# Two f32 stages of a perceiver layer in three passes of split operands, on one Trainium2 core

## The chip, the cores and the metric

The kernel runs on one core of one Trainium2 chip. The metric is the device time of one execution in microseconds; three executions of the kernel before gave 2127.59, 2129.59 and 2129.66 us, so the median is 2129.59.

## What is computed

A perceiver layer: 128 rows of 512 attend to 12544 context rows with 16 heads of 128, then pass a linear attention with a decay per head, then a feed-forward of ternary weights. Each of the three is added to its own input.

```python
def xattn(xn, ctx, Wq, Wk, Wv, Wo):            # H = 16, HD = 128
    q = (xn @ Wq).reshape(b, sq, H, HD) * (1.0 / np.sqrt(HD))
    k = (ctx @ Wk).reshape(b, skv, H, HD)
    v = (ctx @ Wv).reshape(b, skv, H, HD)
    attn = softmax(einsum('bqhd,bkhd->bhqk', q, k))
    return einsum('bhqk,bkhd->bqhd', attn, v).reshape(b, sq, H * HD) @ Wo

def attn(xn, log_decay, Wq, Wk, Wv, Wo, Wg1, Wg2, norm_w):   # 16 heads of 32
    q, k, v = silu(xn @ Wq), silu(xn @ Wk), silu(xn @ Wv)
    o = lightning_attn(q, k, v, log_decay)     # one chunk of 128: (q k^T * D) v
    o = o * sigmoid((xn @ Wg1) @ Wg2)
    return (rms_normed_by_head(o) * norm_w) @ Wo

x = x + xattn(layernorm(x), ctx_2048, ...)
x = x + attn(layernorm(x), ...)
x = x + ffn(layernorm(x), ...)                 # act_quant, ternary w1 and w2
```

## The kernel before

The cross attention is done without ever forming k and v. Wk is multiplied into q first, so that the scores come from the context itself (first loop, line 190), and Wv is applied last, to the weighted sums of the context (`uT`). Both loops hold their f32 operands as two parts: a high part rounded to fp32r by a copy on ScalarE, and a low part, which is the difference, by a subtraction on VectorE. A product is then three fp32r matmuls, low by high, high by low and high by high, added up in PSUM.

The first loop writes the scores to DRAM (`sc_d`), in two halves `f` of the heads. The second loop (the `for k` loop around line 700) takes 2 x 98 = 196 steps. Step k works on one half of a block of 256 context rows: TensorE runs `weigh` for step k (24 matmuls of 512 columns, line 469), while ScalarE and VectorE prepare steps k+1 to k+3: `high_part` and `low_part` (lines 523 and 528), `cut_hi` and `cut_lo` for the context (505, 511), `soften` (517, 518) and the running sum `total` (536). Three buffers for `ph` and `pl` let the preparation run ahead by up to two steps. `load_scores(k + 5)` and `load_ctx(k + 4)` are issued on SyncE's queue.

Work that belongs to no step is put into the loop by `at(k, job)`. The ternary weights of the feed-forward are made there (`stage`, `magnitude`, `quantize`), in four tiles `kq1_0` to `kq1_3` that stay in SBUF until the feed-forward. The weights Wv and Wo of the cross attention are loaded in four groups each, into the rooms `kq1_4` to `kq1_6` in turn, or into score buffers (pool `io`).

After the loop the order of each engine is fixed by hand: `seq` keeps the instructions that it marks in the program's order on their engine. `values(g)` (line 742) multiplies a group of four heads with Wv, in f32, and scales it by the inverse sums into `cT` (line 752). `outs(g)` (line 763) multiplies it with Wo, in f32, 256 columns at a time, onto `po`. The order on TensorE is values 0 and 1, outs 0, values 2, outs 1, values 3, outs 2, outs 3. Beside it VectorE takes the reciprocals of the sums of the second half (line 774), and ScalarE makes the decay matrix (line 799) from `df`, which GpSimd's iota starts (line 793). Then x1 = po + x0 (line 832), its layer norm, its transposition, the three projections of the linear attention in f32 (q and k with the weights stationary, so that they come out transposed, line 853; v at 876), the gate (870, 879), the scores by head (890), the identity matmul that puts x1 under the last sum (897), the weighted values `po2` (906), the gated norm, Wo (932, 935) and the feed-forward. `keep_warm(n)` puts n matmuls of zeros on TensorE where it would stand idle.

Of the kernel before, what the change touches and what calls it, by code (L numbers as in the profile page):

```python
# [8 lines left out]
F32 = mybir.dt.float32  # L9
F32R = mybir.dt.float32r  # L10
BF16 = mybir.dt.bfloat16
# [5 lines left out]
P = 128  # L17
# [16 lines left out]
def tile_perceiver_layer(  # L34
# [546 lines left out]
    w1q = [kq1p.tile([P, 2, FF], BF16, name=f"kq1_{n}") for n in range(2)]  # L581
    w2q = [kq1p.tile([P, 8, D], BF16, name=f"kq1_{n + 2}") for n in range(2)]
    parts = const.tile([P, 2, 8], F32, name="parts")
    staged = {}
# [44 lines left out]

    def score_tile(shape):  # L630

        return iop.tile(shape, F32, tag="io", name="wt")

    def by_cols(w, g, room=weight_tile):

        t = room([P, NC, 512])
        nc.sync.dma_start(out=t, in_=w[:, g * 512 : (g + 1) * 512].rearrange("(c p) e -> p c e", p=P))
        return t

    def by_rows(w, g, room=weight_tile):  # L640

        t = room([P, 4, D])
        nc.sync.dma_start(out=t, in_=w[g * 512 : (g + 1) * 512, :].rearrange("(h p) d -> p h d", p=P))
        return t

    wv, wo = {}, {}
    jobs = {}

    def at(k, job, *args):
        jobs.setdefault(k, []).append((job, args))  # L650
# [18 lines left out]
    for q in range(8):  # L669
        at(2 * NP + 10 + 3 * q, lambda q: seq(nc.vector.reciprocal(rl[0][:, q * P : (q + 1) * P], rl[0][:, q * P : (q + 1) * P])), q)  # L670
    at(2 * NP + 40, lambda: wv.update({0: by_cols(x_wv, 0)}))
    at(2 * NP + 44, lambda: wv.update({1: by_cols(x_wv, 1)}))
    at(2 * NP + 48, lambda: wo.update({0: by_rows(x_wo, 0)}))
    at(4 * NP - 4, lambda: wv.update({2: by_cols(x_wv, 2, score_tile)}))
    at(4 * NP - 3, lambda: wo.update({1: by_rows(x_wo, 1, score_tile)}))

# [59 lines left out]
    def values(g):  # L736
        f, b = g // 2, g % 2
        pc = ps_m.tile([P, G, P], F32, tag="m", name="pc")
        for j in range(G):
            for cc in range(NC):  # L740
                seq(
                    nc.tensor.matmul(  # L742
                        pc[:, j, :],
                        lhsT=wv[g][:, cc, j * HD : (j + 1) * HD],
                        rhs=uT[f][:, cc, b * 512 + j * P : b * 512 + (j + 1) * P],
                        start=(cc == 0),
                        stop=(cc == NC - 1),
                    )
                )
        cTs[g] = work.tile([P, G, P], F32, tag="cT", name="cT", bufs=3)  # L750
        seq(
            nc.vector.tensor_tensor(
                cTs[g].rearrange("p a b -> p (a b)"), pc.rearrange("p a b -> p (a b)"),
                rl[f][:, b * 512 : (b + 1) * 512], ALU.mult,
            )
        )

    def outs(g):
        for half, hs in enumerate(halves):
            for j in range(G):  # L760
                h = g * G + j
                seq(
                    nc.tensor.matmul(  # L763
                        po[half], lhsT=cTs[g][:, j, :], rhs=wo[g][:, j, hs], start=(h == 0), stop=(h == H - 1)
                    )
                )

    ld = small.tile([P, H], F32, tag="ld", name="ld", bufs=1)
    nc.sync.dma_start(out=ld, in_=log_decay.partition_broadcast(P))
    values(0)  # L770
    wv[3] = by_cols(x_wv, 3)
    for q in range(4):
        qs = slice(q * 256, (q + 1) * 256)
        seq(nc.vector.reciprocal(rl[1][:, qs], rl[1][:, qs]))
    values(1)
    wo[2] = by_rows(x_wo, 2)
    outs(0)
    wo[3] = by_rows(x_wo, 3)
    late = [keepp.tile([P, 8, 512], F32, name="uT0")]
    a_w = {"q": by_cols(a_wq, 0, lambda shape: late[0][:, 4:, :])}  # L780
    wg1 = ctp.tile([P, NC, P], F32, tag="hi", name="wg1")
# [8 lines left out]


    di = work.tile([P, P], I32, name="di")
    nc.gpsimd.iota(di, pattern=[[1, P]], base=0, channel_multiplier=-1)
    df = work.tile([P, P], F32, name="df")
    nc.vector.tensor_copy(df, di)
    nc.vector.tensor_scalar_max(df, df, 0.0)
    decay = ctp.tile([P, H, P], F32, tag="raw", name="decay", bufs=1)
    for h in range(H):
        nc.scalar.activation(decay[:, h, :], df, AF.Exp, scale=ld[:, h : h + 1])
    nc.gpsimd.affine_select(  # L800
        out=decay, in_=decay, pattern=[[0, H], [1, P]], compare_op=ALU.is_ge, fill=0.0, base=0, channel_multiplier=-1
    )

    values(2)
    outs(1)
    values(3)
    late.append(keepp.tile([P, 8, 512], F32, name="uT1"))
    a_w["k"] = by_cols(a_wk, 0)
    outs(2)
    a_w["v"] = by_cols(a_wv, 0)  # L810
    outs(3)
    a_w["o"] = by_rows(a_wo, 0)
    rows = {}
# [17 lines left out]
    for half, hs in enumerate(halves):  # L831
        seq(nc.vector.tensor_tensor(x1[:, hs], po[half], x0[:, hs], ALU.add))
        seq(nc.vector.bn_stats(out=st0[:, half, :], in_=x1[:, hs]))
    mv0 = small.tile([P, 2], F32, tag="mv", name="mv0")
    seq(nc.vector.bn_aggr(out=mv0, in_=st0))
# [3 lines left out]
    xa = work.tile([P, D], F32, tag="xa", name="xa")  # L839
    xaT = work.tile([P, NC, P], F32, tag="T", name="xaT", bufs=2)  # L840
    for half, hs in enumerate(halves):
        seq(nc.vector.tensor_scalar(xa[:, hs], x1[:, hs], mv0[:, 0:1], c0, ALU.subtract, ALU.mult))
    for half in range(2):
        transposed(xa, xaT, half)

    def project_T(w):

        pp = ps_m.tile([P, NC, P], F32, tag="m", name="pp")
        for half in range(2):
            for e in range(NC):  # L850
                for cc in (2 * half, 2 * half + 1):
                    seq(
                        nc.tensor.matmul(  # L853
                            pp[:, e, :],
                            lhsT=w[:, cc, e * P : (e + 1) * P],
                            rhs=xaT[:, cc, :],
                            start=(e == 0 and cc == 0),
                            stop=(e == NC - 1 and cc == NC - 1),
                            skip_group_check=True,
                        )  # L860
                    )
        return pp

    qT = late[0][:, 0, :].rearrange("p (e q) -> p e q", e=NC)
    kT = late[1][:, 0, :].rearrange("p (e q) -> p e q", e=NC)
    seq(nc.scalar.activation(qT, project_T(a_w["q"]), AF.Silu))
    seq(nc.scalar.activation(kT, project_T(a_w["k"]), AF.Silu))
    pg = ps_v.tile([P, P], F32, tag="v", name="pg")
    for cc in range(NC):
        seq(nc.tensor.matmul(pg, lhsT=wg1[:, cc, :], rhs=xaT[:, cc, :], start=(cc == 0), stop=(cc == NC - 1)))  # L870
    g1T = work.tile([P, P], F32, tag="g1T", name="g1T")
    seq(nc.vector.tensor_copy(g1T, pg))
    v = late[1][:, 1, :]
    pv = ps_v.tile([P, D], F32, tag="v", name="pv")
    for cc in range(NC):
        seq(nc.tensor.matmul(pv, lhsT=xaT[:, cc, :], rhs=a_w["v"][:, cc, :], start=(cc == 0), stop=(cc == NC - 1)))  # L876
    seq(nc.scalar.activation(v, pv, AF.Silu))
    pgate = ps_v.tile([P, D], F32, tag="v", name="pgate")
    seq(nc.tensor.matmul(pgate, lhsT=g1T, rhs=wg2, start=True, stop=True))
    gate = late[1][:, 2, :]  # L880
    seq(nc.scalar.activation(gate, pgate, AF.Sigmoid))
    seq(nc.scalar.activation(warm, eps_t, AF.Sqrt))


    pscs = [(ps_m, ps_t)[r // 2].tile([P, NC, P], F32, tag="mt"[r // 2], name="psc") for r in range(4)]
    for e in range(NC):
        for r in range(4):
# [6 lines left out]
            )  # L894
    pp = [ps_v.tile([P, 256], F32, tag="v", name="pp") for _ in range(2)]
    for half, hs in enumerate(halves):
        seq(nc.tensor.matmul(pp[half], lhsT=ident, rhs=x1[:, hs], start=True, stop=False))
    po2 = ps_s.tile([P, 512], F32, tag="s", name="po2")
    decayed = decay.rearrange("p (e r) q -> p r e q", r=4)
    for r in range(4):  # L900
        sc = late[1][:, 4 + r, :].rearrange("p (e q) -> p e q", e=NC)
        seq(nc.vector.tensor_tensor(sc, pscs[r], decayed[:, r, :, :], ALU.mult))
        for e in range(NC):

            cs = slice((4 * e + r) * LHD, (4 * e + 4) * LHD)
            seq(nc.tensor.matmul(po2[:, cs], lhsT=sc[:, e, :], rhs=v[:, cs], start=True, stop=True))  # L906
    keep_warm(ps_w, 13)
    og = ctp.tile([P, 2, D], F32, tag="lo", name="og")
# [20 lines left out]
    for i in range(NC):  # L929
        for half, hs in enumerate(halves):  # L930
            if i < 2:
                seq(nc.tensor.matmul(pp[half], lhsT=ogT[:, i, :], rhs=a_w["o"][:, i, hs], start=False, stop=False))  # L932
    for half, hs in enumerate(halves):
        for i in (2, 3):
            seq(nc.tensor.matmul(pp[half], lhsT=ogT[:, i, :], rhs=a_w["o"][:, i, hs], start=False, stop=(i == 3)))
    keep_warm(ps_w, 13)
# [136 lines left out]
    s2, step2 = quant_scales(am5[:, 4:5], others, 1.0)  # L1073
    hq = work.tile([P, FF], BF16, tag="hq", name="hq")
    py = [ps_v.tile([P, 256], F32, tag="v", name="py") for _ in range(2)]
# [94 lines left out]
```

## Time and profile before

| what | us |
|---|---|
| time, median of three | 2129.59 |
| the profiled execution, its time | 2127.83 |
| its span in the profile | 2126.1 |
| TensorE busy | 2112.7 |
| VectorE busy | 1646.7 |
| ScalarE busy | 754.2 |
| first matmul of `values(0)` to the end of `outs(3)` | 2038.96 to 2067.09 |
| first projection matmul to the first of `po2` | 2070.17 to 2085.20 |
| end of the span | 2126.1 |

The page of the profile gives busy time by engine, the span in 40 slices, the costliest groups of instructions (line, engine, operation, tiles, count, busy time, mean of one, idle time before it), and the chain of work that ended last. A matmul's mean is longer than the distance between two of them, since they are pipelined; the distance is read from the chain. An f32 matmul leaves two records, an fp32r one leaves one.

### The profile page before, as it was taken

How to read it: one execution, taken by the hardware profiler on the slowest of the kernel's cores; microseconds unless marked ns; L12 is line 12 of the kernel's file. 1: busy time of each engine (PE TensorE's matmuls, PEld its weight loads, DVE VectorE, ACT ScalarE, POOL GpSimd, SP SyncE). 2: the span in 40 equal slices, each digit the busy share in tenths (PEclk: the TensorE clock that was granted, in tenths of full speed). 3: DMA queues.
4: the chain of work that ended last, by engine and by line, in shares of the span. 5: the costliest groups of instructions: out<-in, count | busy, mean ns of one | idle time of the engine just before them, and what ended most of it. 6: DMA issues, size and time to landing. Idle time of an engine off the chain costs nothing.

```text
span 2126.1 us, 23916 instructions
## 1 busy us (share of the span) xinstructions
PE 2112.7 (99%) x9591; PEld 1745.2 (82%) x9595; DVE 1646.7 (77%) x1827; ACT 754.2 (35%) x846; POOL 25.7 (1%) x15
## 2 busy tenths in 40 slices
PE   8999999999999999999999999999999999999998
PEld 7888888888888888888888888888888888888885
DVE  6877777777777777778897888887788777777745
ACT  6222122211222122214444444444544444444424
POOL 0000000000000000000000000000010000000010
PEclk9999999999999999999999999999999999999999
DMA  5333333333333333336664454553444434444460
GB/s 207 135 140 127 149 141 137 139 129 149 134 144 137 130 149 129 149 151 216 216 238 150 181 179 168 174 202 143 149 149 149 148 142 140 145 142 146 149 230 6
DMA packets 70767, 326.22 MB, mean 153 GB/s; under 512 B 7265, under 2 KB 11617, under 8 KB 45185
## 3 DMA queue, kind: packets, MB, share of 16 engines
q1 hardware_dynamic: 70512, 324.57, 41.4%
q8 instruction: 75, 1.23, 0.2%
q14 instruction: 36, 0.29, 0.1%
q10 hardware_dynamic: 144, 0.13, 0.0%
HBM read 221.65 MB, written 103.02 MB: 153 GB/s over the span
## 4 chain that ended last, share of the span: by engine, by line
PE 98%; DVE 1%; DMA 1%; ACT 0%; SPq 0%; issue 0%; DVEq 0%; ACTq 0%
PE pu L469 50%; PE ps L190 44%; PE pc L742 1%; PE po L763 1%; PE pk L364 1%; DMA kq<-in_x_wq_dram 1%; PE pp L853 0%; PE pq L344 0%; PE po L906 0%; PE pv L876 0%; SPq L300 0%; DVE uT L1057 0%; DVE st L1031 0%; PE pp L932 0%; ACT kq L409 0%
## 5 line engine op out<-in xcount | busy, mean ns | idle before, releaser
L190 PE MATMUL ps<-kq,cth 128*128 128x512 f32 x2744 | 844.5, 389 | 0.0
L469 PE MATMUL pu<-ph,cl 128*128 128x512 f32 x1568 | 610.0, 389 | 0.0
L469 PE MATMUL pu<-pl,ch 128*128 128x512 f32 x1568 | 610.0, 389 | 0.0
L469 PE MATMUL pu<-ph,ch 128*128 128x512 f32 x1568 | 610.0, 389 | 0.0
L190 PEld LDWEIGHTS ps<-kq,cth 128*128 128x128 f32 x2744 | 515.2, 188 | 106.6
L190 PE MATMUL ps<-kq,ctl 128*128 128x512 f32 x1344 | 522.8, 389 | 0.0
L523 ACT CAST ph<-si 128x1024 fp32r<-128x1024 f32 x194 | 203.9, 1051 | 491.9 <-PE pu L469 491.7
L469 PEld LDWEIGHTS pu<-pl,ch 128*128 128x128 f32 x1568 | 294.4, 188 | 61.2
L469 PEld LDWEIGHTS pu<-ph,cl 128*128 128x128 f32 x1568 | 294.4, 188 | 60.9
L469 PEld LDWEIGHTS pu<-ph,ch 128*128 128x128 f32 x1568 | 294.4, 188 | 60.9
L219 DVE TENSOR_TENSOR so<-ps,u 128x512 f32<-128x512 f32 x294 | 202.7, 690 | 134.9 <-PE ps L190 130.5
L190 PEld LDWEIGHTS ps<-kq,ctl 128*128 128x128 f32 x1344 | 252.3, 188 | 52.4
L511 DVE TENSOR_TENSOR cl<-cr,ch 128x1024 fp32r<-128x1024 f32 x98 | 120.2, 1227 | 204.8 <-ACT ch L505 204.8
L254 ACT COPY so<-ps 128x512 f32<-128x512 f32 x98 | 57.6, 588 | 577.6 <-PE ps L190 577.6
L528 DVE TENSOR_TENSOR pl<-si,ph 128x1024 fp32r<-128x1024 f32 x194 | 242.4, 1250 | 1.0 <-ACT ph L523 1.0
L237 DVE TENSOR_TENSOR mx<-mx,so 128x1024 f32<-128x1024 f32 x190 | 232.2, 1222 | 6.7
L517 DVE TENSOR_TENSOR si<-si,mb 128x1024 f32<-128x1024 f32 x194 | 235.7, 1215 | 0.0
L536 DVE TENSOR_TENSOR lsum<-lsum,si 128x1024 f32<-128x1024 f32 x192 | 233.8, 1218 | 0.0
L518 ACT ACTIVATE si<-si 128x1024 f32<-128x1024 f32 x194 | 205.4, 1059 | 60.4 <-DVE si L517 60.4
L505 ACT CAST ch<-cr 128x1024 fp32r<-128x1024 f32 x98 | 102.3, 1044 | 0.0
L176 DVE TENSOR_TENSOR ctl<-ctr,cth 128x1792 fp32r<-128x1792 f32 x47 | 94.9, 2019 | 0.7 <-ACT cth L171 0.7
L171 ACT CAST cth<-ctr 128x1792 fp32r<-128x1792 f32 x48 | 81.7, 1703 | 37.5 <-PE ps L190 35.5
(224 smaller groups left out, 757.8 us busy)
## 6 DMA issues: line engine op xcount, KB each, us to landing
sc<-so SPq DMA_DIRECT2D x98, 1024.0 KB, 3.8
si<-sc SPq DMA_DIRECT2D x97, 1024.0 KB, 5.0
cr<-in_c_dram SPq DMA_DIRECT2D x98, 512.0 KB, 3.5
ctr<-in_cT_dram SPq DMA_DIRECT2D x48, 512.0 KB, 3.5
kq<-in_w1T_dram SPq DMA_DIRECT2D x16, 512.0 KB, 4.3
kq<-in_w2T_dram SPq DMA_DIRECT2D x16, 512.0 KB, 5.0
kq<-in_x_wv_dram SPq DMA_DIRECT2D x3, 1024.0 KB, 5.2
kq<-in_x_wo_dram SPq DMA_DIRECT2D x3, 1024.0 KB, 7.3
```

The costliest lines, as they stand in the source:

```text
L176: return lo, nc.vector.tensor_tensor(lo, raw[:, :7, :, :], hi, ALU.subtract)
L190: nc.tensor.matmul(ps, lhsT=lt[:, a, cc, :], rhs=right(f, b, part)[:, cc, :], start=(first and n == 0), stop=(n == 5), skip_group_check=True,)
L219: place(nc.vector.tensor_tensor(to, t[p], t[q], ALU.add))
L237: place(nc.vector.tensor_tensor(mx[f], mx[f], t["so"][:, j, :], ALU.max))
L469: nc.tensor.matmul(pu[b][cc], lhsT=lt[:, j, cs], rhs=rt[:, bs], start=(first and n == 0), stop=(last and n == 2))
L505: seq(nc.scalar.copy(ctx_hi[f, i], ctx_raw[f, i]))
L511: seq(nc.vector.tensor_tensor(ctx_lo[f, i], ctx_raw[f, i], ctx_hi[f, i], ALU.subtract))
L517: seq(nc.vector.tensor_tensor(exps[k], exps[k], mb[f], ALU.subtract))
L518: seq(nc.scalar.activation(exps[k], exps[k], AF.Exp))
L523: seq(nc.scalar.copy(high[k], exps[k]))
L528: seq(nc.vector.tensor_tensor(low[k], exps[k], high[k], ALU.subtract))
L536: seq(nc.vector.tensor_tensor(lsum[f], lsum[f], exps[k], ALU.add))
```

## The change

Two f32 stages take the form of the loops. `outs` uses the high and the low part of both `cT` and Wo, three fp32r matmuls instead of one f32 matmul. The projections q, k and v use the parts of the transposed x (`xaTh`, `xaTl`) and of their weights, 12 fp32r matmuls of 512 columns each; q and k now come out untransposed, and four transpositions each (`turned`) follow their silu.

The weights are split before they are needed: groups 0 to 2 of Wo inside the second loop (steps 91 to 95, 134 to 138, 142 to 146), group 3 and the three projection weights after it, a quarter (128x512) at a time between the other work of ScalarE and VectorE. The rooms for the parts come from the ternary weights: at step 84 their four tiles are written to DRAM (1 MB each), and they are read back in the stage of the linear attention. The reciprocals of the second half move later, in two pairs; `df` and the decay matrix move earlier; the identity matmul of x1 moves behind `po2`, where seven warm-up matmuls stand instead of 13; `hq` lies in another pool.

```diff
+    ternary_d = [dram.tile([P, 4096], BF16, name=f"ternary{n}") for n in range(4)]
...
+    def ternary(n):
+        return (w1q + w2q)[n].rearrange("p a b -> p (a b)")
+    def put_away(n):
+        nc.sync.dma_start(out=ternary_d[n], in_=ternary(n))
+    def high_quarter(w, hi, lo, q):
+        seq(nc.scalar.copy(hi[q], w[:, q, :]))
+    def low_quarter(w, hi, lo, q):
+        seq(nc.vector.tensor_tensor(lo[q], w[:, q, :], hi[q], ALU.subtract))
+    def quarters(*tiles):
+        return [t[:, q, :] for t in tiles for q in range(4 // len(tiles))]
+    def room(name):
+        return lambda shape, dtype=F32: kq1p.tile(shape, dtype, name=name)
+    def part_in(place):
+        return quarters(place([P, 4, D], F32R))
+    def bring(g, raw_room, hi_room, lo_room):
+        t = by_rows(x_wo, g, raw_room)
+        wo[g] = t, hi_room(), part_in(lo_room)
...
-    at(2 * NP + 40, lambda: wv.update({0: by_cols(x_wv, 0)}))
-    at(2 * NP + 44, lambda: wv.update({1: by_cols(x_wv, 1)}))
-    at(2 * NP + 48, lambda: wo.update({0: by_rows(x_wo, 0)}))
+    for n in range(4):
+        at(84, put_away, n)
+    at(87, lambda: bring(0, room("kq1_4"), lambda: part_in(room("kq1_0")), room("kq1_1")))
+    at(130, lambda: bring(1, room("kq1_5"), lambda: part_in(room("kq1_2")), room("kq1_3")))
+    mx_rooms = lambda: quarters(*[mxp.tile([P, 2, D], F32R, tag=f"mx{n}", name="wh") for n in range(2)])
+    at(137, lambda: bring(2, room("kq1_4"), mx_rooms, room("kq1_6")))
+    for g, k in ((0, 91), (1, 134), (2, 142)):
+        for q in range(4):
+            at(k + q, lambda g, q: high_quarter(*wo[g], q), g, q)
+            at(k + 1 + q, lambda g, q: low_quarter(*wo[g], q), g, q)
+    at(150, lambda: wv.update({0: by_cols(x_wv, 0, room("kq1_5"))}))
+    at(152, lambda: wv.update({1: by_cols(x_wv, 1, room("kq1_4"))}))
     at(4 * NP - 4, lambda: wv.update({2: by_cols(x_wv, 2, score_tile)}))
-    at(4 * NP - 3, lambda: wo.update({1: by_rows(x_wo, 1, score_tile)}))
+    at(4 * NP - 3, lambda: wv.update({3: by_cols(x_wv, 3, score_tile)}))
+    at(4 * NP - 2, lambda: wo.update({3: by_rows(x_wo, 3, lambda shape: ctp.tile(shape, F32, tag="raw", name="w3", bufs=1))}))
...
-        cTs[g] = work.tile([P, G, P], F32, tag="cT", name="cT", bufs=3)
+        cTs[g] = work.tile([P, G, P], F32, tag="cT", name="cT", bufs=1)
...
+    def values_hi(g):
+        hi = work.tile([P, G, P], F32R, tag="Th", name="cTh", bufs=2)
+        seq(nc.scalar.copy(hi, cTs[g]))
+        cTs[g] = hi, cTs[g]
+    def values_lo(g):
+        hi, t = cTs[g]
+        lo = work.tile([P, G, P], F32R, tag="Tl", name="cTl", bufs=2)
+        seq(nc.vector.tensor_tensor(lo, t, hi, ALU.subtract))
+        cTs[g] = hi, lo
     def outs(g):
+        hi, lo = cTs[g]
+        _, whi, wlo = wo[g]
         for half, hs in enumerate(halves):
             for j in range(G):
-                h = g * G + j
-                seq(
-                    nc.tensor.matmul(
-                        po[half], lhsT=cTs[g][:, j, :], rhs=wo[g][:, j, hs], start=(h == 0), stop=(h == H - 1)
+                parts_ = ((lo, whi[j][:, hs]), (hi, wlo[j][:, hs]), (hi, whi[j][:, hs]))
+                for n, (lt, rt) in enumerate(parts_):
+                    seq(
+                        nc.tensor.matmul(
+                            po[half], lhsT=lt[:, j, :], rhs=rt, start=(g == 0 and j == 0 and n == 0),
+                            stop=(g == NG - 1 and j == G - 1 and n == 2),
+                        )
                     )
-                )
...
     ld = small.tile([P, H], F32, tag="ld", name="ld", bufs=1)
     nc.sync.dma_start(out=ld, in_=log_decay.partition_broadcast(P))
-    values(0)
-    wv[3] = by_cols(x_wv, 3)
+    wo[3] = wo[3], part_in(score_tile), None
     for q in range(4):
+        high_quarter(*wo[3], q)
+    di = work.tile([P, P], I32, name="di")
+    nc.gpsimd.iota(di, pattern=[[1, P]], base=0, channel_multiplier=-1)
+    df = work.tile([P, P], F32, name="df")
+    seq(nc.vector.tensor_copy(df, di))
+    seq(nc.vector.tensor_scalar_max(df, df, 0.0))
+    def inverse_sums(q):
         qs = slice(q * 256, (q + 1) * 256)
         seq(nc.vector.reciprocal(rl[1][:, qs], rl[1][:, qs]))
+    values(0)
+    wo[3] = *wo[3][:2], part_in(room("kq1_5"))
+    values_hi(0)
+    low_quarter(*wo[3], 0)
+    values_lo(0)
+    for q in (1, 2):
+        low_quarter(*wo[3], q)
     values(1)
-    wo[2] = by_rows(x_wo, 2)
+    late = [keepp.tile([P, 8, 512], F32, name="uT0")]
+    a_w = {}
+    def split_hi(name, qs=range(4)):
+        for q in qs:
+            high_quarter(*a_w[name], q)
+    def split_lo(name, qs=range(4)):
+        for q in qs:
+            low_quarter(*a_w[name], q)
+    wq_raw = by_cols(a_wq, 0, lambda shape: late[0][:, 4:, :])
+    wk_raw = by_cols(a_wk, 0, room("kq1_4"))
+    low_quarter(*wo[3], 3)
+    values_hi(1)
+    values_lo(1)
+    for h in range(H):
+        seq(nc.scalar.activation(decay[:, h, :], df, AF.Exp, scale=ld[:, h : h + 1]))
...
     outs(0)
-    wo[3] = by_rows(x_wo, 3)
-    late = [keepp.tile([P, 8, 512], F32, name="uT0")]
-    a_w = {"q": by_cols(a_wq, 0, lambda shape: late[0][:, 4:, :])}
+    wv_raw = by_cols(a_wv, 0, room("kq1_0"))
+    a_w["q"] = wq_raw, part_in(room("kq1_1")), None
...
+    inverse_sums(0)
+    inverse_sums(1)
+    split_hi("q")
     values(2)
+    a_w["q"] = *a_w["q"][:2], part_in(score_tile)
+    values_hi(2)
+    values_lo(2)
     outs(1)
+    a_w["k"] = wk_raw, part_in(room("kq1_2")), part_in(room("kq1_3"))
+    inverse_sums(2)
+    inverse_sums(3)
+    split_hi("k")
+    split_lo("q", (0,))
     values(3)
     late.append(keepp.tile([P, 8, 512], F32, name="uT1"))
-    a_w["k"] = by_cols(a_wk, 0)
+    a_w["v"] = wv_raw, part_in(score_tile), None
+    values_hi(3)
+    split_lo("q", (1,))
+    values_lo(3)
+    split_hi("v")
+    split_lo("q", (2, 3))
     outs(2)
-    a_w["v"] = by_cols(a_wv, 0)
+    a_w["v"] = *a_w["v"][:2], part_in(room("kq1_6"))
+    split_lo("k", (0,))
     outs(3)
-    a_w["o"] = by_rows(a_wo, 0)
+    a_wo_t = by_rows(a_wo, 0, room("kq1_5"))
...
+        if half == 0:
+            split_lo("k", (1,))
...
+    xaT = work.tile([P, NC, P], F32, tag="T", name="xaT", bufs=2)
+    xaTh = work.tile([P, NC, P], F32R, tag="Th", name="xaTh", bufs=2)
+    xaTl = work.tile([P, NC, P], F32R, tag="Tl", name="xaTl", bufs=2)
+    ptx = []
     for half in range(2):
-        transposed(xa, xaT, half)
-    def project_T(w):
-        pp = ps_m.tile([P, NC, P], F32, tag="m", name="pp")
+        ptx.append(ps_t.tile([P, 2, P], F32, tag="t", name="pt"))
+        for i in range(2):
+            c_ = (2 * half + i) * P
+            seq(nc.tensor.transpose(ptx[half][:, i, :], xa[:, c_ : c_ + P], ident))
+        seq(nc.scalar.copy(xaTh[:, 2 * half : 2 * half + 2, :], ptx[half]))
+    for half in range(2):
+        cs = slice(2 * half, 2 * half + 2)
+        seq(nc.vector.tensor_tensor(xaTl[:, cs, :], ptx[half], xaTh[:, cs, :], ALU.subtract))
+    split_lo("k", (2, 3))
+    for half in range(2):
+        seq(nc.vector.tensor_copy(xaT[:, 2 * half : 2 * half + 2, :], ptx[half]))
+    split_lo("v")
...
+    def project(name, pool, tag):
+        _, hi, lo = a_w[name]
+        pp = pool.tile([P, D], F32, tag=tag, name="p" + name)
+        turns = []
         for half in range(2):
-            for e in range(NC):
-                for cc in (2 * half, 2 * half + 1):
-                    seq(
-                        nc.tensor.matmul(
-                            pp[:, e, :],
-                            lhsT=w[:, cc, e * P : (e + 1) * P],
-                            rhs=xaT[:, cc, :],
-                            start=(e == 0 and cc == 0),
-                            stop=(e == NC - 1 and cc == NC - 1),
-                            skip_group_check=True,
-                        )
-                    )
-        return pp
+            turns += [(xaTh, cc, hi[cc]) for cc in (2 * half, 2 * half + 1)]
+            turns += [(xaTh, cc, lo[cc]) for cc in (2 * half, 2 * half + 1)]
+        turns += [(xaTl, cc, hi[cc]) for cc in range(NC)]
+        return pp, [
+            lambda n=n, lt=lt, cc=cc, rt=rt: seq(
+                nc.tensor.matmul(pp, lhsT=lt[:, cc, :], rhs=rt, start=(n == 0), stop=(n == len(turns) - 1))
+            )
+            for n, (lt, cc, rt) in enumerate(turns)
+        ]
+    def turned(src, dst):
+        pt = ps_t.tile([P, NC, P], F32, tag="t", name="ptq")
+        for i in range(NC):
+            seq(nc.tensor.transpose(pt[:, i, :], src[:, i * P : (i + 1) * P], ident))
+        seq(nc.scalar.copy(dst[:, 0:2, :], pt[:, 0:2, :]))
+        seq(nc.vector.tensor_copy(dst[:, 2:4, :], pt[:, 2:4, :]))
...
+    flat = {"q": late[0][:, 1, :], "k": late[0][:, 2, :]}
+    for name in "qk":
+        pp, turns = project(name, ps_m, "m")
+        for turn_ in turns:
+            turn_()
+        seq(nc.scalar.activation(flat[name], pp, AF.Silu))
...
+    turned(flat["q"], qT)
+    turned(flat["k"], kT)
...
+    pv, turns = project("v", ps_v, "v")
+    for turn_ in turns[:4]:
+        turn_()
...
+    for turn_ in turns[4:]:
+        turn_()
+    seq(nc.scalar.activation(v, pv, AF.Silu))
+    pgate = ps_v.tile([P, D], F32, tag="v", name="pgate")
+    seq(nc.tensor.matmul(pgate, lhsT=g1T, rhs=wg2, start=True, stop=True))
+    gate = late[1][:, 2, :]
+    seq(nc.scalar.activation(gate, pgate, AF.Sigmoid))
+    seq(nc.scalar.activation(warm, eps_t, AF.Sqrt))
+    w1q = [kq1p.tile([P, 2, FF], BF16, name=f"kq1_{n}") for n in range(2)]
+    w2q = [kq1p.tile([P, 8, D], BF16, name=f"kq1_{n + 2}") for n in range(2)]
+    for n, t in enumerate(w1q + w2q):
+        nc.sync.dma_start(out=t.rearrange("p a b -> p (a b)"), in_=ternary_d[n])
...
-    keep_warm(ps_w, 13)
+    pp = [ps_v.tile([P, 256], F32, tag="v", name="pp") for _ in range(2)]
+    for half, hs in enumerate(halves):
+        seq(nc.tensor.matmul(pp[half], lhsT=ident, rhs=x1[:, hs], start=True, stop=False))
+    keep_warm(ps_w, 7)
...
-    hq = work.tile([P, FF], BF16, tag="hq", name="hq")
+    hq = ctp.tile([P, FF], BF16, tag="raw", name="hq", bufs=1)
```

## The prediction

> **What bounds the kernel now.** I read the page first, then the chain of waits from 2020 us on, then the timelines of TensorE, of VectorE, ScalarE and of SyncE in the same stretch, then the transfers one by one. The page says TensorE sets the time:
>
> ```profile
> PE   8999999999999999999999999999999999999998
> PEclk9999999999999999999999999999999999999999
> ...
> L469 PE MATMUL pu<-ph,ch 128*128 128x512 f32 x1568 | 610.0, 389 | 0.0
> L469 PEld LDWEIGHTS pu<-ph,ch 128*128 128x128 f32 x1568 | 294.4, 188 | 60.9
> ```
>
> PE has no idle time before its main groups (last column), and the clock is full. So in the main loop only a starved PE costs anything. The end is different. The chain of waits in order of time, columns start, duration, what:
>
> ```profile
> 2019.92 19.04 PE pu L469 x84
> 2038.96 7.14 PE pc L742 x64
> 2046.11 3.46 PE po L763 x16
> 2049.57 3.57 PE pc L742 x32
> 2053.14 3.46 PE po L763 x16
> 2056.59 3.57 PE pc L742 x32
> 2060.16 6.92 PE po L763 x32
> 2067.09 0.02 issue
> 2067.11 0.44 DVE x L832
> ...
> 2070.17 7.41 PE pp L853 x64
> 2077.58 0.89 PE pg L870 x8
> 2078.47 3.44 PE pv L876 x8
> 2081.91 0.86 PE pgate L879 x2
> 2082.76 1.10 PE psc L890 x32
> 2083.87 0.63 PE pp L897 x2
> 2084.50 0.00 issue
> 2084.50 0.70 PE pp L897 x2
> 2085.20 3.51 PE po L906 x32
> ```
>
> Nearly all of 2038.96 to 2088.71 is PE work, so a matmul cut here cuts the time, as long as the operands come. A three-pass matmul of 512 columns takes 19.04/84 = 0.2267 us. A plain f32 matmul makes two records: `outs` has eight of 256 columns in 3.46 us (0.4325 each), `values` sixteen of 128 in 3.57 us (0.223).
>
> **What the Trainium skill says.** "FP8 and Floating Point Precision", TensorE Precision Notes: true FP32 takes 4 passes through the array, reduced precision one. The trace agrees: 0.4325 us for 256 columns f32 against 0.2267 for 512 of fp32r. "TensorE: Matmul & The Clock Gate", LDWEIGHTS: a load costs its column count over 1.2, 107 ns for 128. The trace has the loads at 188 ns, but the records of `values` load weights every 3.57/32 = 0.112 us, so loads of about 107 ns are hidden back to back. "DMA: Bandwidth & Descriptors", Queues, rings and completion order: each DMA engine consumes descriptors in ring order. The trace agrees: the loads issued at 2046.14, 2046.57 and 2049.60 land after 5.5, 7.8 and 7.5 us, at 2051.6, 2054.4 and 2057.1, one every 2.7 us. "Advanced Engine Details and Errata", GPSIMD Details: Pool shares a port with DVE and conflicts where DVE has two SBUF inputs. The trace agrees once: a 128x1024 low part took 2.92 us instead of 1.22 beside an all-reduce.
>
> **The change, part by part.** T is counted from 2038.96, the start of `values(0)`.
>
> *Main loop.* Added: four 1 MB writes of the ternary weights at step 84, the splits of wo 0 to 2 (12 ScalarE copies, 12 VectorE subtractions of 128x512), and the loads of wv and wo at other steps. A VectorE step of 5.44 us holds 3.5 operations of 1.14 = 4.0 us; one subtraction is about 0.60 (half of 1.14 plus overhead). Covered: 0. The writes matter more. They stand in SyncE's queue behind the context load issued at 1433.06 and before the scores load at 1435.33, which VectorE wants at 1446.70. Score writes in the first loop run at 442 GB/s when busy, so 4 MB take 10, the context half and the scores 4.1, fixed latency some 2.3: landing near 1449.4, 2.7 us late. Behind that wait stand the low part of step 89 and everything later on VectorE. Before, it was done at 1450.76; PE wants it at 1457.0. So the lateness is covered, with 3 us left. I take 0; it would cost lateness minus 6.
>
> *Output projection.* Removed: 32 f32 matmuls, 4 x 3.46 = 13.84. Added: 96 of fp32r with 256 columns. This shape is not in the trace. Below: half of 0.2267 = 0.1133; with the whole 13 ns surplus of the 512 shape over 213 ns kept: 0.120. Far bound: no faster than 512 columns, 0.2267. I take 0.1165: 24 x 0.1165 = 2.80 a group, 11.2 in all. PE ends at 4 x 3.57 + 11.2 = T+25.5, against T+28.15.
>
> But the operands now pass through two engines. Durations: ScalarE copy of 512, 0.60, one every 0.52 (1.05 and 0.95 at 1024); VectorE subtraction 0.69, one every 0.60; cT 0.69; reciprocal 6.58/4 = 1.645; decay 4.78.
> - cT1 at 7.16 when `values(1)` is done; its high part 7.87 to 8.47; low part to 9.09; two reciprocals to 12.4. The high part of q waits on its weights, requested at 7.2 and landed near 12.6.
> - ScalarE: decay 8.5 to 13.3, high parts of q to 15.4, then the high part of cT2 (cT2 ready at 14.2) to 15.96; its low part on VectorE 15.98 to 16.58.
> - VectorE: two reciprocals to 19.87, one q low part to 20.47, cT3 to 21.09 (PE has it at 19.9), low part of cT3 seen at 22.45; PE wants it at 22.7. No stall, margin 0.25.
> - VectorE then: two q lows and one k low to 24.2, x1's first half and its statistics to 25.08, one k low to 25.68, x1's second half at 25.68. Before: 28.15.
>
> So VectorE, not PE, ends this stage, by 0.2: gain 2.47. The iota that df needs waits for GpSimd, whose 7.18 us gap before it stays; it now begins after the first memset (2034.2), so iota at 2041.4 = T+2.4, ahead of cT0 at T+3.6.
>
> *Projections.* T0 is the first projection matmul, 3.06 after x1's second half as before (ScalarE's first copy is the same; the second copy, 0.4 later, is wanted 0.9 later). Before, from T0 to po2: 15.03. Now: q and k 2 x 12 x 0.2267 = 5.44; gate input 0.89; eight transposes, 0.127 each from four in 0.67, so 1.02 (0.9 to 1.2); v's first four 0.91; scores 1.10; v's other eight 1.81; pgate 0.86: 12.03. Gain 3.00. k's low parts are done at T0+2.05 (wanted at 4.1), v's at 5.25 (wanted at 7.9); the silu of v ends at 11.8 against po2 at 12.0; the sigmoid ends at 13.7 against po2's end at 15.5. The identity matmul of x1 moves behind po2, where 3.06 us until the transposes held 2.75 of warm-up; 0.86 plus seven of 0.215 is 2.4. Cost 0.
>
> *Ternary weights back.* Four 1 MB loads, the first requested at T0+5.3 behind three others, landing 2.7 apart up to T0+22 at the latest; w1 is wanted at T0+27. The fourth stands behind row_lb, which waits for v at T0+11. Cost 0; the cover is 5 us or more. hq's new place: 0.
>
> Sum: 2.47 + 3.00 = 5.47, rounded to 5.4. The profiled execution took 2127.83 (span 2126.10 and 1.73 around it), so 2122.4; it lies 1.76 below the median of 2129.59, which gives 2124.2.
>
> **The rivals.**
> - *The splits set the stage.* ScalarE and VectorE form one chain from cT1 to x1 with no air. For it: the margin of 0.25 at the last group, q's weights landing 0.7 before use, and Pool's affine_select (2.02) beside VectorE. If q's weights land 2 us late, or iota keeps its old T+7.8 place (3.8 later), x1 comes 2 to 4 us later: gain 3.4 to 1.5, about 2126.8, which is the same within what can be told. Against it: the 5.2 us landing on an empty queue.
> - *A 256-column fp32r matmul costs what one of 512 costs.* Place: line 763. Then 96 x 0.2267 = 21.8 instead of 13.84: 7.9 lost, 3.0 won, 2134.5, slower. It decides from 0.175 us per matmul (16.84/96) on; slower by 0.2% from 0.22. Against it: 128-column records load weights every 0.112.
> - *The 4 MB write starves PE at step 89.* If writes and reads mixed get 250 GB/s, the scores land some 9 us late, 3 lost: 2127.2, the same. For: one queue in order. Against: 442 GB/s.
>
> **How the numbers follow.** What can be told from no change here is 0.2%, 4.26 us; my 5.4 clears it by little. Forecast 0.62; splits 0.24; starved PE 0.07; slow 256 columns 0.07. Within the forecast case 0.03 falls under 4.26, and a mild split case gives 0.05 to faster: faster 0.64, within 0.2% 0.29, slower 0.07. The forecast's own range is 2122.7 to 2125.3 (matmul 0.1133 to 0.120, transposes, 0.5 on the VectorE chain). For 8 in 10 it reaches over most of the split cases: 2122.5 to 2128.
>
> **What would show it.** Right: `outs` groups of 2.7 to 2.9 us; x1's second half at T+25.7 with VectorE busy before it; 12.0 us from the first projection matmul to po2; no PE idle in step 89. Wrong: groups over 4 us; iota after T+3.6; q's high copies starting after T+13.3; a gap on PE near 1457.

## The result, and the profile after

Over twelve runs each, the kernel before took 2128.43 us (2127.59 to 2129.69) and the changed kernel 2123.81 us (2122.85 to 2125.03): 4.62 us less, ratio 0.9976 with a 95% interval of 0.9968 to 0.9983 (the ratio is not the quotient of the two medians, which is 0.9978). The profiled execution took 2123.22 us, of which the span is 2121.5; before it was 2127.83 and 2126.1. The forecast was 2124.2.

The chain of waits of the changed kernel, in order of time (start, duration, what):

```profile
2039.06 7.14 PE pc L782 x64
2046.20 2.88 PE po L817 x24
2049.08 3.57 PE pc L782 x32
2052.65 2.87 PE po L817 x24
2055.52 3.57 PE pc L782 x32
2059.10 4.33 PE po L817 x36
2063.42 0.02 issue
2063.45 0.43 DVE x L929
...
2068.00 3.01 PE pq L971 x12
2071.01 2.72 PE pk L971 x12
2073.73 0.89 PE pg L993 x8
2074.62 0.87 PE ptq L979 x8
2075.49 0.92 PE pv L971 x4
2076.42 1.15 PE psc L1009 x32
2077.57 2.05 PE pv L971 x8
2079.62 0.86 PE pgate L1018 x2
2080.48 3.60 PE po L1034 x32
```

Read it against the chain before, which the prediction shows, from three marks: T, where `values(0)` starts; T0, the first projection matmul; and po2, the attention's output (`po` of L1034, L906 before). The fall of the span, 4.6 us, splits without a remainder:

| stretch | before | after | fall | predicted |
|---|---|---|---|---|
| start of the span to T | 2038.96 | 2039.06 | -0.10 | 0 |
| T to T0 (output projection, norm) | 31.21 | 28.94 | 2.27 | 2.47 |
| T0 to po2 (q, k, v, scores, gate) | 15.03 | 12.48 | 2.55 | 3.00 |
| po2 to the end of the span | 40.90 | 41.02 | -0.12 | 0 |

The -0.10 of the first row is within what T varies: in the ten profiles with this loop (the changed kernel, E1, and E4 to E11) it lies between 2038.24 and 2039.66. Of the -0.12 of the last row, 0.09 is `po` itself, which took 3.60 us instead of 3.51.

A group of `outs` went from 3.46 to 2.88 us; its 24 matmuls take 0.120 us each. The last two groups stand in the chain as one entry, with 36 of their 48 matmuls, because the chain leaves TensorE when the first half of `po` is done. VectorE's timeline shows what follows (start, duration, line, operation, tiles):

```profile
2062.70 0.68 DVE L661 TENSOR_TENSOR kq<-kq,kq 128x512 fp32r<-128x512 f32 x1
2063.45 0.42 DVE L929 TENSOR_TENSOR x<-po,x 128x256 f32<-128x256 f32 x1
2063.91 0.43 DVE L930 BATCH_NORM_STATS2 st<-x 128x6 f32<-128x256 f32 x1
2064.25 0.67 DVE L661 TENSOR_TENSOR kq<-kq,kq 128x512 fp32r<-128x512 f32 x1
2064.88 0.42 DVE L929 TENSOR_TENSOR x<-po,x 128x256 f32<-128x256 f32 x1
```

Where nothing holds it up, an instruction of VectorE here begins some 0.08 us before the record of the one ahead of it ends (2064.25 against 2063.91 + 0.43), so the low part of k's weight begun at 2064.25 lets x1's second half start at about 2064.85. TensorE's last matmul of the group ends at 2059.10 + 5.76 = 2064.86 (48 matmuls of 0.120). The two engines arrive within what the trace can tell: which of them sets the stage can't be read here, and the runs E7, E10 and E11 are about that.

The four writes of ternary weights were not where the prediction had put them. SyncE's own row for them (minimum/median/maximum of issuing, first and last start):

```profile
L654 SPq DMA_DIRECT2D ternary<-kq x4: 326/442/461, 1218.8 to 1414.3; - x4
```

They are spread over 195 us: each was placed in SyncE's order as soon as its tile was quantized, not at step 84 (about 1433 us), where the source has them.

### The profile page after: what moved, and what is told of

Its sections match the earlier page's. It is cut to its first block, busy times and chain, and to the rows that moved or that the text cites. A ratio compares the mean times of both kernels' runs of the same rounds, so it can differ in the third digit from the quotient of the medians.

```text
span 2121.5 us, 23998 instructions
## 1 busy us (share of the span) xinstructions
PE 2108.5 (99%) x9590; PEld 1743.4 (82%) x9593; DVE 1668.7 (79%) x1864; ACT 772.1 (36%) x881; POOL 25.6 (1%) x15
## 4 chain that ended last, share of the span: by engine, by line
PE 97%; DVE 1%; DMA 1%; ACT 0%; SPq 0%; issue 0%; DVEq 0%; ACTq 0%
PE pu L469 50%; PE ps L190 44%; PE pc L782 1%; PE pk L364 1%; DMA kq<-in_x_wq_dram 1%; PE po L817 0%; PE pq L344 0%; PE po L1034 0%; SPq L300 0%; PE pq L971 0%; PE pv L971 0%; PE pk L971 0%; DVE uT L1188 0%; DVE st L1162 0%; PE pp L1063 0%
```

## The experiments

The kernel before was run beside each set: medians 2128.82 (E1 to E4), 2129.12 (E5 to E8), 2129.17 (E9 to E11) and 2128.43 (E12). Ratios are to it, as recorded; the quotient of the medians differs from them by up to 0.0002. Lines of code that are left out between others are marked by "...".

### E1 and E2: one half of the change each

E1 keeps the three-pass output projection and puts the f32 projections back; E2 does the opposite.

```diff
 # E1
-    a_w["q"] = wq_raw, part_in(room("kq1_1")), None
...
-    split_hi("q")
...
+    seq(nc.scalar.activation(qT, project_T(a_w["q"]), AF.Silu))
 # E2
-            at(k + q, lambda g, q: high_quarter(*wo[g], q), g, q)
...
+                        po[half], lhsT=cTs[g][:, j, :], rhs=wo[g][:, j, hs], start=(h == 0), stop=(h == H - 1)
...
-    values_hi(0)
```

> The output projection of the cross attention in three passes, as in the changed kernel; the attention's projections q, k and v in plain f32 with xaT first, as before; no q, k, v splits. Theory (the gain is two separate terms): from values(0) to the start of the 128-row x transposes 28.9 us as in the changed kernel (before 31.2), from there to the first po matmul of the attention's output (L1034 in the changed kernel) 15.0 as before: 2.3 us below before, 2126.1, ratio 0.9989. Rival 'VectorE's splits set the stage': with the splits of q, k and v gone, VectorE reaches x1 some us earlier and the stage ends earlier than 28.9, so over 3 us below before. Rival 'the whole gain comes from the projections': ratio 1.000.

> q, k and v in three passes with their weights split ahead as in the changed kernel; the output projection of the cross attention in plain f32 with unsplit Wo, as before (no cT and Wo splits). Theory: 31.2 us from values(0) to the transposes as before, 12.5 from there to the attention's po as in the changed kernel (before 15.0): 2.5 us below before, 2125.9, ratio 0.9988. With the run of the output projection alone the two falls should add to the 4.6 of the changed kernel within 0.5. Rival (the parts only work together, since one gives buffers or time to the other): the two falls add to less than 3.5 or more than 6.

E1: 2126.65 us, ratio 0.9989 (0.9981 to 0.9997). E2: 2126.44, 0.9989 (0.9982 to 0.9995). The falls are 2.17 and 2.38 us, together 4.55, against 4.62 for the whole change. The profiles give the same: E1 has 28.89 from T to T0 and 15.04 from T0 to po2, E2 has 31.20 and 12.55. So the gain is two independent terms, as the prediction had it. E1 also bears on the rival that the splits set the stage: without the splits of q, k and v it needs 28.89, as much as with them, so they cost nothing beyond what TensorE needs anyway.

### E3: the four writes in one burst

A copy of a part of each ternary tile onto itself at step 83 keeps the writes from starting earlier.

```diff
+    def touched(n):
+        seq(nc.vector.tensor_copy(ternary(n)[:, :512], ternary(n)[:, :512]))
+    for n in range(4):
+        at(83, touched, n)
```

> The changed kernel with one 512-column copy of each ternary tile onto itself on VectorE at step 83, so that the four put-aways of 1 MB cannot start when their tiles are quantized (1218 to 1414 us in the changed kernel) and go in one burst near step 84; nothing left out. Theory: the next score tiles land about 3 us late, within the 3 us by which they are early: no TensorE gap, time as the changed kernel within 0.2% (2123.8), plus at most 1 us for the four copies. Rival 'the 4 MB write starves TensorE': a TensorE gap of about 3 us in steps 84 to 90, 2127.

Measured 2124.20 us, ratio 0.9979 (0.9971 to 0.9987): as the changed kernel. The writes now stand close together, in two pairs. SyncE's timeline of E3:

```profile
1429.35 0.80 SPq L654 DMA_DIRECT2D ternary<-kq  x2
1434.35 0.33 SPq L499 DMA_DIRECT2D cr<-in_c_dram  x1
1434.73 0.93 SPq L654 DMA_DIRECT2D ternary<-kq  x2
1436.62 0.51 SPq L493 DMA_DIRECT2D si<-sc  x1
```

The transfers issued between 1434.9 and 1440 us (KB each, median time to landing), and below them TensorE in windows of E3 (window, length, busy, clock as a share of full speed, DMA share, GB/s; the last two windows are for the section on E9 and E12):

```profile
ternary<-kq SPq DMA_DIRECT2D x2, 1024.0 KB, 7.8
si<-sc SPq DMA_DIRECT2D x1, 1024.0 KB, 10.4
```

```profile
1425.00:1470.00 45.00, 45.00 (x200) 1.00 0.65 244
...
2107.00:2110.00 3.00, 1.86 (x3) 0.68 0.01 3
2110.00:2113.00 3.00, 3.00 (x8) 0.75 0.00 0
```

The scores behind the burst landed 10.4 us after their issue, at 1447.0; the median of the same load in the kernel before is 5.0. VectorE wanted them at 1447.99, so the 5.4 us were covered with 1.0 us left, and TensorE was busy 45.00 of 45.00 us. This burst is harmless, and in the changed kernel it does not even arise. It is milder than the one in the prediction, though: two of the writes were issued at 1429.35, ahead of the context load, and not all four between that load and the scores. That stronger burst was not run.

### E4: the iota late

The blocks that clear the gate weights on GpSimd, with the loads that belong to them, stand ahead of the iota instead of behind it.

```diff
+    seq(nc.gpsimd.memset(wg1, 0.0))
...
+    seq(nc.gpsimd.memset(wg2, 0.0))
...
     di = work.tile([P, P], I32, name="di")
-    nc.gpsimd.iota(di, pattern=[[1, P]], base=0, channel_multiplier=-1)
+    seq(nc.gpsimd.iota(di, pattern=[[1, P]], base=0, channel_multiplier=-1))
```

> The changed kernel with the iota for the decay put behind the two memsets of the gate weights on GpSimd, with nothing else moved; nothing left out. Theory: the iota starts behind the memsets, which wait for buffers of the value matmuls, at about 7.8 us after values(0) instead of 2.6; VectorE, in whose order the df copy stands ahead of the first cT normalization, waits for it, so cT0 and with it outs(0) is 3 to 5 us later, and not all of it is made up: 2 to 4 us over the changed kernel, 2126 to 2128. Rival (the decay is off the path, VectorE makes the delay up in its idle time): as the changed kernel, within 0.5 us.

Measured 2129.18 us (2126.54 to 2132.65), ratio 1.0003 (0.9995 to 1.0011): the whole gain is gone, and more was lost than expected. GpSimd's timeline, first of the changed kernel, then of E4; "issue" is idle time that waits for nothing in the trace:

```profile
2033.68 0.60 POOL L875 MEMSET wg<- 128x512 f32 x1
2041.64 0.23 POOL L830 IOTA di<- 128x128 int32 x1 [7.37 <-issue]
```

```profile
2038.75 0.52 POOL L833 MEMSET wg<- 128x512 f32 x1 [4.90 <-PE pu L469]
2046.04 0.23 POOL L840 IOTA di<- 128x128 int32 x1 [6.76 <-issue]
```

The first iota of the stage comes some 7 us after whatever stands ahead of it on GpSimd. TensorE in windows of E4:

```profile
2038.65:2046.00 7.35, 7.13 (x64) 1.00 0.05 12
2046.00:2049.00 3.00, 0.17 (x1) 1.00 0.53 162
2049.00:2053.00 4.00, 4.00 (x25) 0.68 1.00 388
2053.00:2057.00 4.00, 4.00 (x34) 0.90 0.55 205
```

T to T0 is 33.78 us, 4.84 more than in the changed kernel. `outs(0)` starts at 2048.83, 10.2 after T instead of 7.1: 3.0 of wait, which was expected. The other 1.8 is the clock: after the pause it stood at 0.68 of full speed, and `outs(0)` took 4.26 us instead of 2.88, the next `values` 3.99 instead of 3.57. In this execution the stall cost 1.6 times its own length.

The other executions of E4 agree. Each lists the mean clock that TensorE was granted, as a share of full speed. In two of the 13 it is 1.000, and they took 2126.54 and 2126.86 us, some 3.2 above the runs of the changed kernel with that clock (median 2123.53): the wait alone. In four it is 0.999 (2127.35 to 2129.18 us), in seven 0.998 (2128.82 to 2132.65 us). So the prediction's point that the iota must come before T+3.6 was right, and so was its price of 2 to 4 us for the old place as far as the wait goes; the clock behind the wait was not in it. It is the place in the change that carries most risk.

### E5 and E6: the width of a matmul

E5 cuts each 256-column matmul of `outs` into two of 128. E6 does groups 0 to 2 with 512 columns, for which both halves of `po` are put into one tile, and moves two low parts of k behind x1.

```diff
 # E5
+        for quarter in range(4):
+            half, hs = quarter // 2, slice(quarter * P, (quarter + 1) * P)
 # E6
+    whole_po = ps_s.tile([P, 512], F32, tag="s", name="po")
...
+        for hs in halves if g == NG - 1 else [slice(0, 512)]:
```

> The changed kernel with each 256-column matmul of the output projection cut in two of 128 columns (192 instead of 96, same products). Theory 'a matmul has a fixed floor from its weight load': each 128-column one takes 0.11 to 0.12 us like the 256-column one, a group 5.4 to 5.8 instead of 2.88, the stage 10 us longer, 2133 to 2135. Rival 'time goes with the columns': 0.06 each, a group 2.9 to 3.0, as the changed kernel within 0.5 us.

> The changed kernel with groups 0 to 2 of the output projection in matmuls of 512 columns into one bank (12 a group at 0.2267 = 2.72 instead of 24 at 0.120 = 2.88), the last group in halves as it is, and the first two low quarters of k moved on VectorE behind x1. Theory (TensorE and VectorE end the stage together, and both are made shorter): 3 x 0.16 = 0.5 us below the changed kernel, 2123.3. Rival (the cT normalizations or ScalarE's copies gate the groups): 0.1 or less.

E5: 2133.43 us, ratio 1.0020 (1.0013 to 1.0028). The chain of E5 has its first group as

```profile
2046.68 5.31 PE po L819 x48
```

which is 0.1106 us for each of 48 matmuls. With 0.120 at 256 columns and 0.2267 at 512, the cost has a floor of about 0.11 us, and 256 columns stand just above it. The Trainium skill ("TensorE: Matmul & The Clock Gate", LDWEIGHTS) prices a weight load at its columns over 1.2, which for 128 columns makes an estimate of 107 ns; the floor measured here lies some 4 ns above that, so the weight load is its likely cause, though no run took the load away.

E6: 2124.43 us, 0.9980 (0.9973 to 0.9988): not faster than the changed kernel (0.9976). T to T0 rose from 28.94 to 29.64. VectorE's timeline of E6:

```profile
2061.59 1.28 DVE L661 TENSOR_TENSOR wt<-uT,kq 128x512 fp32r<-128x512 f32 x2
2064.89 0.42 DVE L929 TENSOR_TENSOR x<-po,x 128x256 f32<-128x256 f32 x1 [2.01 <-PE po L818]
2065.35 0.43 DVE L930 BATCH_NORM_STATS2 st<-x 128x6 f32<-128x256 f32 x1
2065.69 0.41 DVE L929 TENSOR_TENSOR x<-po,x 128x256 f32<-128x256 f32 x1
```

Groups of twelve did take some 2.73 us, but x1's first half now starts at 2064.89, when the second half of `po` is done too: with both halves in one tile, the early half is no longer released early. In the changed kernel it starts 1.43 ahead of the second. The low part of cT3 also came just behind TensorE, which began the last group at 2061.73, though its matmul ahead had begun at 2061.25 and 0.23 is the step. What was won on TensorE (3 x 0.15) was more than given back in the hand-over.

### E7, E10 and E11: TensorE, VectorE, or both

VectorE's "list" is here the work that stands ahead of x1 in its fixed order. E7 leaves out the two products of the output projection that have a low part; it is a probe, since the full product is no longer computed. E10 moves two low parts of k behind x1. E11 does both and is a probe too.

```diff
 # E7, E11
-            parts_ = ((lo, whi[j][:, hs]), (hi, wlo[j][:, hs]), (hi, whi[j][:, hs]))
+            parts_ = ((hi, whi[j][:, hs]),)
...
 # E10, E11
-    split_lo("k", (0,))
     outs(3)
...
-        if half == 0:
-            split_lo("k", (1,))
...
-    split_lo("k", (2, 3))
+    split_lo("k")
```

> The changed kernel with only the high x high product of the output projection on TensorE; the two products with a low part are left out (64 of 96 matmuls), all splits are still made. Theory (VectorE's list reaches x1 together with TensorE): 7.7 us of TensorE work less give under 0.3 us. Rival 'TensorE alone sets the stage': up to 2.9 us less (the last cT at 20.4 us after values(0), then one group of 8 at 0.120), 2121.

> The changed kernel with the first two low quarters of k's weight moved on VectorE behind x1 (0.6 us each off VectorE's list ahead of x1); nothing left out. Theory (TensorE and VectorE reach the end of the stage together): x1's halves still wait for TensorE, from values(0) to the transposes 28.9 us as in the changed kernel, no change in time. Rival 'VectorE's list alone sets the stage': 0.6 to 1.2 us less.

> Both at once: the k quarters moved behind x1, and only the high x high product of the output projection on TensorE (the two products with a low part are left out). Theory: with TensorE's 7.7 us alone the stage fell by 0.2, with VectorE's 1.2 alone by nothing, with both it falls by 1.2 to 1.4, to 27.5 to 27.7 us. Rival (the cT3 normalization or ScalarE's copies are a third limit right behind): less than 0.5, 28.4 or more.

| | us | ratio (interval) | T to T0 |
|---|---|---|---|
| changed kernel | 2123.81 | 0.9976 (0.9968 to 0.9983) | 28.94 |
| E7, TensorE 7.7 us less | 2123.50 | 0.9975 (0.9965 to 0.9986) | 28.72 |
| E10, VectorE 1.2 us less | 2124.14 | 0.9976 (0.9968 to 0.9985) | 28.94 |
| E11, both | 2122.62 | 0.9970 (0.9959 to 0.9981) | 27.52 |

The times lie within each other's intervals; the stretch from T to T0, free of what happens elsewhere, decides. Neither engine alone is worth more than 0.22 us, both together 1.42. VectorE in E7, in E10 and in E11:

```profile
2061.87 0.68 DVE L661 TENSOR_TENSOR kq<-kq,kq 128x512 fp32r<-128x512 f32 x1
2062.47 0.41 DVE L929 TENSOR_TENSOR x<-po,x 128x256 f32<-128x256 f32 x1
```

```profile
2063.82 0.42 DVE L928 TENSOR_TENSOR x<-po,x 128x256 f32<-128x256 f32 x1 [0.67 <-PE po L817]
2064.28 0.43 DVE L929 BATCH_NORM_STATS2 st<-x 128x6 f32<-128x256 f32 x1
2065.26 0.42 DVE L928 TENSOR_TENSOR x<-po,x 128x256 f32<-128x256 f32 x1 [0.55 <-PE po L817]
```

```profile
2061.40 1.29 DVE L661 TENSOR_TENSOR wt<-uT,kq 128x512 fp32r<-128x512 f32 x2
2062.61 0.41 DVE L928 TENSOR_TENSOR x<-po,x 128x256 f32<-128x256 f32 x1
```

In E7 x1 follows k's low part with no idle time: the list rules. TensorE was done at 2062.16, 1.7 us before x1's second half began, although the clock fell there too: it had waited 4.63 us, and the eight matmuls of the last group took 2.08 us, not the 0.96 of eight at 0.120. In E10 VectorE idles 0.67 and 0.55 us for TensorE: the list is short, and TensorE rules. In E11 the list rules again, 1.2 us earlier. That is a tie between two engines.

### E8: v in one piece

E8 is E6 with all twelve matmuls of v ahead of the score matmuls.

```diff
-    for turn_ in turns[:4]:
+    for turn_ in turns:
         turn_()
+    seq(nc.scalar.activation(v, pv, AF.Silu))
...
-    for turn_ in turns[4:]:
-        turn_()
-    seq(nc.scalar.activation(v, pv, AF.Silu))
```

> The 512-column groups and the moved k quarters of the run e6, and all twelve matmuls of v ahead of the score matmuls instead of four ahead and eight behind. Theory: v's second part loses its re-entry (2.05 instead of 1.81 for eight), 0.2 us more than e6's fall: 0.7 us below the changed kernel, 2123.1. Rival: the score matmuls come 1.8 us later, the scores' masking on VectorE and with it the attention's po is later by more than that: at or above the changed kernel.

Measured 2124.52 us, 0.9980 (0.9972 to 0.9989). T0 to po2 is 12.40 instead of 12.48: most of the 0.2 expected did not come. The chain of E8:

```profile
2076.76 2.73 PE pv L969 x12
2079.50 1.10 PE psc L1008 x32
2080.60 1.05 PE pgate L1014 x2
```

The twelve took 2.73 us, down from 0.92 + 2.05 = 2.97, but the gate's matmuls, which now follow the score matmuls, took 1.05 instead of 0.86. The price of coming after those matmuls, which work on 32 rows, went to the next in line.

### E9 and E12: the clock in the tail

The spans of E1, E3 and E4 held 1.2 us more than their stages explain: from po2 to the first `py` matmul it was 34.4 to 34.5 us, against 33.2 before and 33.3 after. The groups of TensorE (busy, mean ns, idle before, releaser) show six f32 matmuls that differ, first in the changed kernel, then in E3:

```profile
L1193 PE MATMUL pn<-uT,diagonal 128*128 128x512 f32 x6 | 2.8, 605 | 2.2 <-ACT diagonal L1191 2.2
```

```profile
L1198 PE MATMUL pn<-uT,diagonal 128*128 128x512 f32 x6 | 4.5, 906 | 2.2 <-ACT diagonal L1196 2.2
```

Same work, same pause of 2.2 us, and in E3 a clock of 0.68 and 0.75 (the last two windows shown there). E1, E4, E6, E7 and E10 had it too: six of the twelve profiled executions with this pause. E9 fills the pause in the changed kernel, E12 in the kernel before:

```diff
-    keep_warm(ps_w, 12)
+    keep_warm(ps_w, 21)
     rh = col("rh")
```

> The changed kernel with 21 instead of 12 of the warming matmuls ahead of the six f32 matmuls of L1193 (pn), so that TensorE's pause of 2.17 us before them shrinks to about 0.1; nothing left out. Theory (in a part of the runs that pause makes the clock fall, and pn then takes 4.48 us instead of 2.81, which puts it on the chain and lengthens the tail by 1.2 us): the slow tail does not come any more, the lowest time stays as it is, the median falls by 0.3 to 0.8 us to about 2123.2, and the runs spread over less than now. Rival (the clock falls for another reason, such as what the chip has drawn before): pn at 4.48 us in some runs as before, median as the changed kernel's.

> The kernel before with 21 instead of 12 warming matmuls ahead of the six f32 matmuls of its L1062 (pn), the edit of the run e9; nothing left out. Theory (the slow tail is of the clock and comes to both kernels, the change has no part in it): the median falls by 0.3 to 0.8 us below before's of the same runs, the spread gets smaller as it did in e9, and the changed kernel with the same edit stays 4 to 5.5 us below this one. Rival (the change itself brings the slow tail, or takes it away): no fall here, and the difference of the two warmed kernels is under 4 or over 6 us.

E9: 2123.31 us (2122.73 to 2123.83, 8 runs), ratio 0.9972 (0.9962 to 0.9982). It is the lowest median of a kernel here that leaves nothing out. E12: 2127.89 (2126.99 to 2129.28), 0.9997 (0.9988 to 1.0005). In both profiles the pause is 0.2 to 0.3 us and `pn` takes 2.8. Each median is 0.5 us lower, as expected, but E12's interval takes in no fall, E9's overlaps the changed kernel's, and only E9's spread got smaller (1.1 us from lowest to highest, against 2.2 of the changed kernel).

The mean clock that each run lists says more. A clock of 0.68 and 0.75 over 6 us takes 0.0008 from the mean, so such a run shows as 0.999, as the profiles of E1, E3, E6 and E10 do.

| | runs at 1.000, their median | runs at 0.999, their median |
|---|---|---|
| changed kernel | 7, 2123.53 us | 5, 2124.50 us |
| E9, the pause filled | 8 of 8, 2123.31 | none |
| kernel before, beside E12 | 10, 2128.23 | 7, 2129.25 |
| E12, the pause filled | 13 of 13, 2127.89 | none |

Beside E9, 15 of 21 runs of the kernel before list 0.999. So the pause is what lets the clock fall, and a run in which it falls is about 1.0 us longer. What filling it saves on the median hangs on how many runs would have had the fall; the 0.5 us are not settled by these intervals. The two warmed kernels are 4.58 us apart, so the clock has no part in the change's gain.

## Why the prediction was right

The forecast case came true, with the parts where it had put them: two gains, one in each stage, and nothing lost in the main loop. But the gain was set too high. The sum had 5.47, taken as 5.4; it came out as 4.6 between the profiles and 4.62 between the medians.

That the forecast time of 2124.2 still lies within 0.4 us of the measured 2123.81 is partly luck. It was counted from a median of three runs, 2129.59, and twelve runs put the kernel before at 2128.43, which is 1.16 lower. That error and the 0.8 us too much of gain cancel for the most part.

- *Main loop, 0.* Right (-0.10 us), for another reason. The step put the four writes at step 84 and had the scores land 2.7 us late. In the changed kernel the writes are spread over 1218.8 to 1414.3 us. E3 made a milder burst: the scores came 1.0 us before they were wanted, not late. The lateness itself was never run.
- *Output projection, 2.47; measured 2.27.* The 256-column matmul was taken at 0.1165 between bounds of 0.1133 and 0.120; it takes 0.120. Over 96 that is 0.34, which brings TensorE from T+25.5 to T+25.80. VectorE's list was given T+25.68 and came at T+25.82. The sentence "VectorE, not PE, ends this stage, by 0.2" was wrong in that it named one: with 0.120 they tie (E7, E10, E11). From x1's second half to T0 it took 3.12, not 3.06. The iota was at T+2.58 against T+2.4, in time for cT0.
- *Projections, 3.00; measured 2.55.* The path of 12.03 came out as 12.48. q took 3.01 instead of 2.72, where k, right behind it with the same twelve, took 2.72: q's first matmul comes after a wait; v's other eight took 2.05 instead of 1.81, since they follow the score matmuls (E8); the scores took 1.15 instead of 1.10. The transposes were better, 0.87 instead of 1.02. Together 0.43 of the 0.45 missing. A steady rate was used for groups that begin anew.
- *Ternary weights back, 0.* Right: T0 to po2 and the tail show no wait for them. The loads landed in 9.0 us at the median, with the queue moving 403 GB/s.
- *The rivals.* Slow 256-column matmuls: refuted by 2.88 a group; E5 shows the same thing one size down, where 128 columns cost nearly what 256 do. Starved TensorE: no wait of TensorE in the main loop of the changed kernel, and none around the burst of E3; the stronger burst stays untried. Splits that set the stage: they are as late as TensorE, no later, and E4 shows what their one weak point, the iota, would have cost. The conflict of GpSimd with VectorE, read in the prediction from one subtraction (2.92 us instead of 1.22 beside the all-reduce that starts at 1446.88), is a weak reading: the subtraction ahead of it, begun at 1446.70 and with both operands in SBUF too, took 1.22.

## What to carry to other kernels

Price a chain of fp32r matmuls by its floor as well as by its columns (here about 0.11 us each, so that 256 columns cost hardly more than 128), and add some 0.2 to 0.3 us for each group that starts after a wait or after matmuls of another row size. When two engines reach the end of a stage together, relieving one shows next to nothing: take work from each alone and then from both before calling either the limit. Follow TensorE's pauses of 2 us and more as far as the clock behind them, since the wait is not the whole price.

## What the runs showed of the hardware

- A pause of 2.2 us on TensorE let the clock fall in six of twelve profiled executions, and in none of the 21 runs of E9 and E12, where it is filled. In the profiles of E4, E7 and E11 it fell after pauses of 3.0, 4.63 and 4.63 us as well. The Trainium skill ("TensorE: Matmul & The Clock Gate", What's actually happening) speaks of an idle window of about 3.4 us that runs free of the program; shorter pauses than that were enough here. That it came in only half of the executions would fit a window that runs free, but no run here shows the window.
- The first iota came 6.8 to 7.4 us after the GpSimd instruction ahead of it, with nothing to wait for in the trace, in the kernel before, the changed kernel and E4 alike. What fills that time, the traces do not show.
